# Attention plus feed-forward on one core: first values made beside keys and queries, queries split straight from PSUM, stacked copies moved in halves, last tiles in another order

## The chip, the cores and the metric

One core of a Trainium2 chip runs the whole program in one launch. Its engines are named as in the profile: PE (TensorE matmuls) and PEld (its weight loads), DVE (VectorE), ACT (ScalarE), POOL (GpSimd) and SP (SyncE, which here only issues DMAs). The metric is the device time of one execution in microseconds; lower is better.

## What is computed

The reference, cut to what matters (x is 2 x 1024 x 512, all float32, 16 heads of 32):

```python
qkv  = einsum('bsd,ed->bse', x, w_qkv) + b_qkv          # q, k, v: 2 x 16 x 1024 x 32
s    = einsum('bhqd,bhkd->bhqk', q, k) / sqrt(32)        # causal mask above the diagonal
out  = einsum('bhqk,bhkd->bhqd', softmax(s), v)          # heads side by side: 2 x 1024 x 512
x    = layernorm(x + einsum('bsd,ed->bse', out, w_out) + b_out)
h    = relu(einsum('bsd,hd->bsh', x, sign(up_weight)) * up_scale)           # 2048 wide
x    = layernorm(x + einsum('bsh,dh->bsd', h, sign(down_weight)) * down_scale * output_scale)
```

## The kernel before

**A planner writes the order.** Every step is a `task` with the engines that may run it, the modelled time it takes, a `place` (a due time, in units of one 128x128 block of attention scores) and the parts of tiles that it reads and writes. `Plan.schedule` (L133) walks through modelled time and, whenever an engine is free, gives it the ripe task with the lowest place. What it yields is one fixed order of instructions per engine. On the chip each engine runs its own list in that order and waits where an operand isn't there yet; SP's list of DMAs is such a queue too. A DMA takes one of 8 lanes (L50): the ninth is issued when the first has landed.

**Chunks.** There are 8 chunks `(b, e)`: batch b, and a group e of 4 heads (128 columns). A chunk has 8 query tiles of 128 rows; tile i looks at i+1 key blocks, so a chunk has 36 places (`STEP`, L496). While the attention of one chunk runs, `project` (L677) makes keys, queries and values of the next; the loop at L1285 sets the places.

**Projection.** `product` (L549) makes 128 features x 512 positions of keys or queries with 8 fp32 matmul passes (L554). Scores aren't multiplied in fp32: each number is split into a rounded part `hi` and a rest `lo` (both fp32r), and the four pairings of hi and lo are laid on top of each other over 128 partitions, once for each head (the "stacks"). Keys are split straight from PSUM, `split_keys` (L627): one ACT pass (L633) and one DVE pass (L638). Queries take three: `with_bias` (L570) writes a full copy with bias and scale on DVE (L575), and `split` (L612) makes hi and lo of it on POOL (L616, L621). `stack` (L645) then moves them with 16 DMAs for keys and 16 for queries, 1024 positions (128 KB) each; in the traces these are the lines `stacks<-wqkv`, issued by SP at L510. `values_of` (L585) makes the values, 512 positions at a time (L591).

**Attention.** `scores` (L810): matmuls into a PSUM tile of two banks (L847; the first four tiles of chunk 0 use plain fp32, L828), mask and row maximum on DVE (L885), exponential on ACT (L900), reciprocal on DVE (L912), scaling on POOL (L918). `transposes` (L930) turns blocks of 128x128 on PE (L939) and copies them to SBUF on ACT or DVE (L492, L494), into a ring `pt` of 60 blocks; a tile that doesn't fit before the ring's end starts at its beginning. `values` (L956) multiplies by the values (L968). After a batch's last chunk `output` (L1018) does the output projection (L1033) and the residual, and `normalise` (L1056) the layer norm (L1076).

**Start and end of the program.** `first_half` (L705) loads the first chunk's weights and the first 512 positions of x, in 128-row pieces c = 0 to 3, and multiplies keys and queries piece by piece (L755). Five tiny DVE copies (`hold`, L697) keep the values' weights and the second half of x from being issued before the first piece of x has landed. `second_half` (L786) makes the rest of chunk 0. The feed-forward (L1131) runs in 4 blocks of 512 rows; in the last one the output of a tile of 128 rows goes through L1225 (scale), L1234 (residual), L1242 and L1250 (statistics), L1257 (root), L1263 (reciprocal), L1268 (normalise) and a DMA of 256 KB. The last tile is made in two halves of 256 columns.

Of the kernel before, what the change touches and what calls it, by code (L numbers as in the profile page):

```python
# [11 lines left out]
F32R = mybir.dt.float32r  # L12
# [18 lines left out]
LAST = [0, 1, 2, 7, 6, 5, 4, 3]  # L31
# [43 lines left out]
class Plan:  # L75
# [8 lines left out]
    def ring(self, cls, n):  # L84

        self.classes[cls] = {"tiles": [], "next": 0, "ring": n, "live": [], "at": 0.0}

    def room(self, c, x):

        live, n = c["live"], x.blocks  # L90
        if not live:
            return 0
        head, tail = live[-1].slot + live[-1].blocks, live[0].slot
        if head > tail:
            return head if head + n <= c["ring"] else 0 if n <= tail else None
        return head if head + n <= tail else None
# [180 lines left out]
def kernel(  # L277
# [87 lines left out]
    def place_for(stack, name, n, kind=F32, side="left"):  # L365
# [22 lines left out]
        "hl": views(a_h, (2, S), F32R),  # L388
        "full": views(a_h, (TB,), at=2 * S),
# [70 lines left out]
    for cls, (_, n) in rings.items():  # L460
        plan.ring(cls, n)
# [25 lines left out]
    DMA = {"SP": (0.6, 0.6)}  # L487
# [43 lines left out]

    def load_w(b, e, place, parts, queue=DMA, after=()):
# [3 lines left out]
        for n in parts:  # L536
# [10 lines left out]
            )  # L547

# [21 lines left out]
    def with_bias(b, e, n, dst, parts, ps, at):  # L570
        bias = bqk[:, n * NC + e : n * NC + e + 1]
        if n == 0:
            plan.task(
                dve(0.74),
                lambda _: nc.vector.tensor_scalar(dst(), bank(ps), bias, scale, ALU.add, ALU.mult),  # L575
                at, [ps[0]], parts, label="bias",
            )
        else:
            plan.task(
                act(0.69),  # L580
                lambda _: nc.scalar.activation(dst(), bank(ps), AF.Identity, bias=bias),
                at, [ps[0]], parts, label="bias",
            )

    def values_of(b, e, v, t0, place):  # L585

        xt, w, ps = inputs[b], weights[b, e], new("f")
        for t in range(4):
            for c in range(NC):
                def fn(_, t=t, c=c):  # L590
# [10 lines left out]
                    [xt[c, t0], w[2]],  # L601
# [25 lines left out]
    def split_keys(b, e, hl, at, ps, place):  # L627

        bias = bqk[:, NC + e : NC + e + 1]
# [47 lines left out]
    def project(b, e, lo, mid, hi):  # L677
# [3 lines left out]
        for n in (1, 0):  # L681
            hl = new("hl")
            for t0 in range(0, S, TB):
                ps = product(b, e, n, t0, place)
                if n:
                    split_keys(b, e, hl, t0, ps, place() - FAST)
                else:
                    full = new("full")
                    with_bias(b, e, 0, lambda full=full: of(full), [full[0]], ps, place() - FAST)
                    split(hl, t0, lambda full=full: of(full), [full[0]], place())  # L690
            stack(st, n, hl, 0, 0, S, place, DMA)
        place = pace(mid, hi, 32)
# [3 lines left out]

    def hold(src, parts, dst, held):  # L697

        for d, h in zip(dst, held):
            plan.task(  # L700
                dve(0.15), lambda _, d=d: nc.vector.tensor_copy(d(), src()), -200, parts, [h],
                label="hold",
            )

    def first_half():  # L705
# [13 lines left out]
        for c, z, n in ((0, 1, 1), (0, 1, 0), (1, NC, 1), (1, NC, 0)):  # L719
            dma(  # L720
                -100,
                lambda c=c, z=z, n=n: of(w)[:, c:z, n, :],
                lambda c=c, z=z, n=n: w_qkvT[c * P : z * P, n * D : n * D + P].rearrange(
                    "(c p) f -> p c f", p=P
                ),
                64 * (z - c),
                writes=[w[n, k] for k in range(c, z)],
                queue=act_queue,
            )
            if n == 0 and c == 0:  # L730
                dma(-100, lambda: bqk, lambda: b_qkvP, 8, writes=[biases[0]], queue=act_queue)
        xt = inputs[0] = new("xT")
        for c in range(NC):
            dma(
# [6 lines left out]
        hold(  # L741
            lambda: of(xt)[:, 0, 0:1], [xt[0, 0]],
            [lambda: of(w)[:, 0, 2, 0:1], *[lambda c=c: of(xt)[:, c, TB : TB + 1] for c in range(NC)]],
            [w[2], *[xt[c, TB] for c in range(NC)]],
        )
        load_w(0, 0, -90, [2])
# [3 lines left out]
        both = {n: new("f") for n in (1, 0)}  # L750
        for c in range(NC):
            for n in (1, 0):
# [9 lines left out]
                    -50, [xt[c, 0], w[n, c]], updates=[both[n][0]], count=2,  # L762
                    label="ps",
                )
        for n in (1, 0):
            bias = bqk[:, n * NC : n * NC + 1]
            if n == 0:
# [3 lines left out]
                        rows(0), bank(both[0]), bias, scale, ALU.add, ALU.mult  # L771
# [11 lines left out]
        values_of(0, 0, v, 0, lambda units=0: -1)  # L783
        plain[0, 0] = kq, v

    def second_half():  # L786

        kq, v = plain[0, 0]
        st, hl = new("st"), new("hl")
        place = pace(-10, 6, 16 * 3)  # L790
        split(hl, 0, lambda: of(kq)[:, TB : 2 * TB], [kq[1]], -20)
        stack(st, 1, hl, 0, 0, TB, lambda: -20)
        ps = product(0, 0, 1, TB, place)
        split_keys(0, 0, hl, TB, ps, -10)
        stack(st, 1, hl, TB, TB, TB, lambda: -20)
        ps = product(0, 0, 0, TB, place)
        qh, full = new("hl"), new("full")
        with_bias(0, 0, 0, lambda: of(full), [full[0]], ps, -10)
        split(qh, 0, lambda: of(full), [full[0]], -10)
# [10 lines left out]
    def scores(b, e, i, heads, at):  # L810
# [86 lines left out]
        for j in range(G):  # L897
            plan.task(
# [31 lines left out]
    def transposes(i, heads, pr, at):  # L930
        blocks = [(j, ts(j * (i + 1) + k, P)) for j in range(len(heads)) for k in range(i + 1)]
        pt = new("pt", blocks=len(blocks))
# [198 lines left out]
    def feed_forward(up, dn, dsc, base):  # L1131
        UNIT = 2.0

        def block(tb):
# [80 lines left out]
            for t in range(TPB):  # L1215
# [3 lines left out]
                if very:  # L1219
                    at -= 23  # L1220
# [179 lines left out]
```

## Time and profile before

| | |
|---|---|
| median of 3 runs | 760.41 us (759.64 to 761.68) |
| the profiled execution | 761.84 us |
| its span, first to last instruction | 759.0 us |
| granted TensorE clock over the span | 0.997 |
| busy: PE, PEld, DVE, ACT, POOL | 745.2, 575.7, 476.3, 377.2, 267.3 us |
| SP's DMA issues of stacks | 224 of 128 KB, 48 of 64 KB |

How to read it: the profiled execution is one execution; 2.84 us of it lie outside the span. The attention part takes the first 505 us, the feed-forward the rest. In the groups of instructions the columns are line, engine, operation, output<-input, shapes and count, then busy time, mean ns of one, and the engine's idle time just before them with what ended it. In the timeline they are start, length of the merged group, engine, line, operation and count, and in brackets the idle time before it and who ended it. "SPq" is SP's queue of DMA issues.

### The profile page before, as it was taken

What the parts mean: (1) busy time and instruction counts of PE and PEld (TensorE: products, weight loads), DVE (VectorE), ACT (ScalarE), POOL (GpSimd) and SP (SyncE); (2) the same over time, 40 slices, a digit from 0 to 9 for tenths busy, and PEclk for the clock granted to TensorE, in tenths of its full rate; (3) what the DMA queues carried; (4) which work ended last, traced back from release to release, by engine and by line L of the source; (5) the groups of instructions that cost most, each with busy time, mean ns of one, the idle gap of its engine ahead of it and who ended that gap; (6) DMA issues with size and microseconds to landing.
All of it is one profiled execution on the core that took longest, in us unless ns stands there. A gap on an engine that the chain in (4) does not pass through costs nothing.

```text
span 759.0 us, 15486 instructions
## 1 busy us (share of the span) xinstructions
PE 745.2 (98%) x5890; PEld 575.7 (76%) x5890; DVE 476.3 (63%) x1146; ACT 377.2 (50%) x848; POOL 267.3 (35%) x333
## 2 busy tenths in 40 slices
PE   8999999999999999999999999999999999999995
PEld 4668869769757776886977977668787787778884
DVE  1657787787755767777778769744346337336525
ACT  1448776766642755687676767823222222222210
POOL 2416445445535453554544555520011002002005
PEclk9999999999999999999999999999999999999998
DMA  6577346057354125514505534241001001000101
GB/s 183 127 161 156 114 105 143 18 112 182 99 126 119 49 71 112 124 31 102 123 2 111 126 112 154 84 148 61 1 0 57 1 0 56 0 1 2 56 0 55
DMA packets 38216, 62.35 MB, mean 82 GB/s; under 512 B 6144, under 2 KB 18432, under 8 KB 38144
## 3 DMA queue, kind: packets, MB, share of 16 engines
q1 hardware_dynamic: 36912, 60.85, 31.1%
q8 instruction: 46, 0.75, 0.4%
q10 hardware_dynamic: 1232, 0.53, 0.3%
q14 instruction: 26, 0.21, 0.1%
HBM read 24.66 MB, written 4.19 MB: 38 GB/s over the span
## 4 chain that ended last, share of the span: by engine, by line
PE 90%; DVE 4%; DMA 2%; SPq 1%; POOL 1%; issue 1%; ACT 0%; POOLq 0%; ACTq 0%; DVEq 0%
PE s L939 15%; PE s L1153 15%; PE pd L1197 14%; PE s L554 13%; PE d L847 9%; PE s L968 8%; PE s L1033 7%; PE s L591 7%; SPq L510 1%; PE s L1101 1%; DMA xT<-in_xT 1%; PE d L828 1%; DVE x L1076 1%; DVE atT L1225 1%; DVE small L1242 1%
## 5 line engine op out<-in xcount | busy, mean ns | idle before, releaser
L918 POOL TENSOR_SCALAR probs<-probs,small 128x128 f32<-128x128 f32 (+7 forms) x256 | 189.0, 748 | 234.4 <-DVE small L912 160.6
L900 ACT ACTIVATE probs<-d,small 128x128 f32<-128x128 f32 (+7 forms) x256 | 189.3, 748 | 46.9 <-DVE small L912 17.7
L885 DVE CUSTOM_DVE_ANT_0 d<-d,mask 128x384 f32<-128x384 f32 (+7 forms) x200 | 173.3, 877 | 27.1 <-PE d L847 23.9
L939 PE MATMUL s<-ident,probs 128*128 128x128 f32 x1152 | 162.8, 273 | 1.3 <-DVE probsT L494 1.0
L939 PEld LDWEIGHTS s<-ident,probs 128*128 128x128 f32 x1152 | 135.7, 140 | 33.1 <-issue 22.4
L492 ACT COPY probsT<-s 128x512 f32<-128x512 f32 (+3 forms) x205 | 100.5, 519 | 117.6 <-PE s L939 113.8
L1153 PE MATMUL s<-xt,stacks 128*128 128x512 f32 x512 | 133.1, 400 | 0.0
L1197 PE MATMUL pd<-stacks,hid 128*128 128x512 f32 (+1 forms) x512 | 131.8, 392 | 0.6 <-DVE hid L1170 0.6
L1164 ACT ACTIVATE hf<-s,ups 128x512 f32<-128x512 f32 x64 | 44.0, 688 | 160.2 <-PE s L1153 158.2
L847 PE MATMUL d<-stacks 128*128 128x512 f32 (+3 forms) x368 | 121.3, 423 | 1.4 <-ACT probs L900 0.9
L554 PE MATMUL s<-xT,wqkv 128*128 128x512 f32 x240 | 118.6, 595 | 0.0
L1153 PEld LDWEIGHTS s<-xt,stacks 128*128 128x128 f32 x512 | 94.4, 188 | 23.7 <-issue 1.0
L1197 PEld LDWEIGHTS pd<-stacks,hid 128*128 128x128 f32 x512 | 92.7, 188 | 22.6 <-DVE hid L1170 1.5
L1170 DVE CAST hid<-hf 128x512 fp32r<-128x512 f32 x64 | 27.4, 428 | 121.7 <-ACT hf L1164 121.7
L494 DVE COPY probsT<-s 128x512 f32<-128x512 f32 (+3 forms) x140 | 82.2, 595 | 21.5 <-PE s L939 17.4
L847 PEld LDWEIGHTS d<-stacks 128*128 128x128 f32 x368 | 59.8, 190 | 36.9 <-issue 20.6
L591 PE MATMUL s<-wqkv,xT 128*128 128x128 f32 x512 | 75.3, 276 | 0.0
L591 PEld LDWEIGHTS s<-wqkv,xT 128*128 128x128 f32 x512 | 67.7, 191 | 7.2 <-issue 6.1
L968 PE MATMUL s<-probsT,v 128*32 128x128 f32 x2304 | 68.7, 274 | 0.0
L968 PEld LDWEIGHTS s<-probsT,v 128*32 128x32 f32 x2304 | 61.2, 110 | 9.6 <-DVE small L912 2.4
L1033 PE MATMUL s<-wout,atT 128*128 128x512 f32 x128 | 63.4, 594 | 0.0
L554 PEld LDWEIGHTS s<-xT,wqkv 128*128 128x128 f32 x240 | 39.4, 190 | 18.7 <-issue 17.4
(72 smaller groups left out, 521.9 us busy)
## 6 DMA issues: line engine op xcount, KB each, us to landing
stacks<-wqkv SPq DMA_DIRECT2D x224, 128.0 KB, 2.4
wqkv<-in_w_qkvT SPq DMA_DIRECT2D x22, 256.0 KB, 3.7
xT<-in_xT SPq DMA_DIRECT2D x16, 256.0 KB, 4.6
rows<-in_x SPq DMA_DIRECT2D x16, 256.0 KB, 2.6
raw<-in_up_wT SPq DMA_DIRECT2D x4, 1024.0 KB, 5.1
out<-atT SPq DMA_DIRECT2D x16, 256.0 KB, 2.0
stacks<-wqkv SPq DMA_DIRECT2D x48, 64.0 KB, 2.0
raw<-in_down_wT SPq DMA_DIRECT2D x2, 1024.0 KB, 5.1
```

Source lines behind the costliest of these rows:

```text
L492: nc.scalar.copy(dst, src)
L554: nc.tensor.matmul(of(ps).rearrange("p a b -> p (a b)"), lhsT=of(w)[:, c, n, :], rhs=of(xt)[:, c, t0 : t0 + TB], start=(c == 0), stop=(c = ...
L591: nc.tensor.matmul(of(ps)[:, t, :], lhsT=of(xt)[:, c, t0 + t * P : t0 + (t + 1) * P], rhs=of(w)[:, c, 2, :], start=(c == 0), stop=(c == NC ...
L847: nc.tensor.matmul(of(sc)[:, at0 : at0 + k1 - k0], lhsT=of(st)[:, 0, u, ts(i, P)], rhs=of(st)[:, 1, u, k0:k1], start=True, stop=True,)
L885: lambda _, j=j, some=some: nc.vector.tensor_tensor_reduce(some(), some(), keys(mask[:, S - N :], 0, N), scale=-1.0, scalar=LARGEST, op0=A ...
L900: lambda _, j=j: nc.scalar.activation(keys(of(pr), j, N), keys(of(sc), j, W), AF.Exp, bias=of(nm)[:, j : j + 1], scale=sign, accum_out=of( ...
L918: lambda _, j=j: nc.gpsimd.tensor_scalar(of(pr)[:, j * N : (j + 1) * N], of(pr)[:, j * N : (j + 1) * N], of(sums)[:, j : j + 1], 1.0, ALU. ...
L939: lambda _, k=k, c=c, tp=tp: nc.tensor.transpose(of(tp)[:, k, :], of(pr)[:, c], ident),
L968: nc.tensor.matmul(of(to)[ts(u, HD), n, :], lhsT=of(v)[:, k, ts(u, HD)], rhs=of(pt)[:, ts(c + k, P)], start=(k == i), stop=(k == 0),)
L1033: lambda _, c=c: nc.tensor.matmul(bank(py), lhsT=of(a)[:, c, :], rhs=of(wout)[:, c, :], start=(c == 0), stop=(c == NC - 1),),
L1153: lambda _, f=f, c=c, n=n, pu=pu: nc.tensor.matmul(of(pu), lhsT=of(up)[:, f // TPB, c, ts(f % TPB, P)], rhs=of(xt)[:, n, c, :], start=(c = ...
L1197: lambda _: nc.tensor.matmul(of(to)[:, d0:d1], lhsT=of(h)[:, ts(t, P)], rhs=of(dn)[:, f // 4, f % 4, d0:d1], start=(f == 0 and n == 0), st ...
```

## The change

- `first_half`: weights come by piece c, keys' and queries' together; piece 0 goes over ACT's queue, pieces 1 to 3 over SP's just ahead of the same piece of x. The values of the first 512 positions are multiplied piece by piece too, into a bank of their own, in places after keys and queries. `hold` is gone; the values' weights of pieces 1 to 3 follow the last piece of x, then x's second half.
- Queries are split from PSUM as keys are (`split_bank`: ACT, then DVE). The factor 1/sqrt(32) is put into the queries' weights by one POOL pass for each chunk (`scaled`) and into the bias once. `with_bias` is gone.
- `hl` holds 512 positions, and there are three of them; `stack` is called for each 512 positions: 64 DMAs of 64 KB for a chunk in place of 32 of 128 KB.
- During chunk 0, chunk 1's values come first (places 0 to 12), its keys and queries in places 4 to 24, its weights earlier.
- The ring `pt` may wrap inside a tile; a group of 4 blocks that lies across its end is copied in two pieces.
- The first batch's 8 layer-norm steps move into chunk 4, each behind a tile's exponential.
- The last chunk's tiles run in the order 2, 7, 6, 5, 4, 3, 1, 0 (before: 0, 1, 2, 7, 6, 5, 4, 3).
- In the last feed-forward block, each tile's closing steps have places of their own (the tile before the last closes after the last); the normalising step is on DVE, the residual add on DVE or POOL as the planner finds, and the last tile's two halves are normalised and sent separately, the first over ACT's queue.

```diff
-LAST = [0, 1, 2, 7, 6, 5, 4, 3]
+LAST = [2, 7, 6, 5, 4, 3, 1, 0]
...
     def room(self, c, x):
+        if c["wraps"]:
+            return head % c["ring"] if sum(y.blocks for y in live) + x.blocks <= c["ring"] else None
...
-        "hl": views(a_h, (2, S), F32R),
-        "full": views(a_h, (TB,), at=2 * S),
+        "hl": views(a_h, (2, TB), F32R),
...
-    DMA = {"SP": (0.6, 0.6)}
+    DMA = {"SP": (0.64, 0.64)}
...
+    def scaled(w, place, parts):
+        plan.task(
+            pool(0.69),
+            lambda _: nc.gpsimd.tensor_scalar(
+                of(w)[:, :, 0, :], of(w)[:, :, 0, :], scale, 1.0, ALU.mult, ALU.mult
+            ),
+            place, updates=[w[p] for p in parts], label="scale",
+        )
...
     def load_w(b, e, place, parts, queue=DMA, after=()):
+            if n == 0:
+                scaled(t, place + 10, [0])
...
-    def split_keys(b, e, hl, at, ps, place):
-        bias = bqk[:, NC + e : NC + e + 1]
+    def split_bank(b, e, n, hl, at, ps, place):
+        bias = bqk[:, n * NC + e : n * NC + e + 1]
...
-    def project(b, e, lo, mid, hi):
+    def project(b, e, lo, mid, hi, values=None):
         for n in (1, 0):
-            hl = new("hl")
             for t0 in range(0, S, TB):
+                hl = new("hl")
                 ps = product(b, e, n, t0, place)
-                if n:
-                    split_keys(b, e, hl, t0, ps, place() - FAST)
-                else:
-                    full = new("full")
-                    with_bias(b, e, 0, lambda full=full: of(full), [full[0]], ps, place() - FAST)
-                    split(hl, t0, lambda full=full: of(full), [full[0]], place())
-            stack(st, n, hl, 0, 0, S, place, DMA)
-        place = pace(mid, hi, 32)
+                split_bank(b, e, n, hl, 0, ps, place() - FAST)
+                stack(st, n, hl, t0, 0, TB, place)
+        place = pace(mid if values is None else values, hi, 32)
...
+        weight(0, 1, 1, act_queue)
+        weight(0, 0, 1, act_queue)
+        dma(-100, lambda: bqk, lambda: b_qkvP, 8, writes=[biases[0]], queue=act_queue)
+        weight(0, 2, 1, act_queue)
         for c in range(NC):
+            if c:
+                weight(c, 0, 2, DMA)
             dma(-100, lambda c=c: of(xt)[:, c, :TB], lambda c=c: xT[ts(c, P), :TB], 256, ...)
-        hold(...)
-        load_w(0, 0, -90, [2])
+        for c in range(1, NC):
+            weight(c, 2, 1, DMA)
         load_x(0, -80, [TB])
...
-                    -50, [xt[c, 0], w[n, c]], updates=[both[n][0]], count=2,
+                    c - 50, [xt[c, 0], w[n, c]], updates=[both[n][0]], count=2,
+            for t in range(TB // P):
+                plan.task(
+                    {"PE": (0.218, 0.218)},
+                    lambda _, c=c, t=t: nc.tensor.matmul(
+                        of(vs)[:, t, :], lhsT=of(xt)[:, c, ts(t, P)], rhs=of(w)[:, c, 2, :],
+                        start=(c == 0 and t == 0), stop=(c == NC - 1 and t == TB // P - 1),
+                    ),
+                    c - 40, [xt[c, 0], w[2, c]], updates=[vs[0]], count=2, label="ps_v",
+                )
...
     def second_half():
+        scaled(weights[0, 0], -30, [(0, c) for c in range(NC)])
...
+        if b and e == 0:
+            normalise(b - 1, base + 18, [marks[b, e, (NQ + t) // 2] for t in range(NQ)])
...
+            if at == 0:
+                load_w(nb, ne, base - 25, [2, 1, 0], after=[latest["x"]])
+                project(nb, ne, base + 4, base + 24, base + 12, base)
+            else:
+                load_w(nb, ne, base - 15, [1, 0, 2])
+                project(nb, ne, base, base + MID * STEP, base + HI * STEP)
...
+                if final:
+                    at += 3 * t - 30
+                later = at + (20 if final and t + 2 == TPB else 0)
...
-                    pool(0.69) if final and not very else dve(0.546),
+                for k, (_, d0, d1) in enumerate(columns(t)):
+                        dve(0.546 if whole else 0.32),
...
+                    dma(at, ..., reads=[y[d0]],
+                        queue=DMA if whole or k else {"ACT": (0.65, 0.65)}, label="out")
-        ADDS = {False: [pool(1.264)] * 3 + [dve(0.692)], True: [pool(1.264)] * 3}
+        either = {**dve(0.692), **pool(1.264)}
+        ADDS = {False: [pool(1.264)] * 3 + [dve(0.692)], True: [either] * 3}
```

## The prediction

> **What bounds the kernel now.** I read the page's first section, then the table of PE's waits, then the timeline at the start, at one change of chunk and at the end.
>
> ```profile
> PE 745.2 (98%) x5890; PEld 575.7 (76%) x5890; DVE 476.3 (63%) x1146; ACT 377.2 (50%) x848; POOL 267.3 (35%) x333
> ```
> ```profile
> PE s L712 <- DVE x L708: 1.0, 1, 1.0
> PE s L755 <- DMA xT<-in_xT: 1.0, 1, 1.0
> PE s L939 <- DVE probsT L494: 1.0, 2, 0.7
> PE d L847 <- ACT probs L900: 0.9, 2, 0.7
> PE pd L1197 <- DVE hid L1170: 0.6, 2, 0.3
> PE d L847 <- DMA stacks<-wqkv: 0.5, 1, 0.5
> ```
> PE is the bound nearly everywhere: its waits (columns: total, times, longest) come to under 6 us. A busy PE may still stand behind an operand, so I laid each matmul's start against the back-to-back spacing of its own form (0.429 us for an fp32 pass of 512 columns, 0.109 for 128, 0.232 for an fp32r pass, 1.72/4 and 3.41/120 in merged groups, and so on). Those spacings sum to 729.6 us of work; from the first matmul (1.04) to the last one's end (751.2) there are 20.6 us of slack. 8.1 of these lie before 54 us, some 10 in pieces of 0.1 where PE changes its kind of matmul, 3.2 between 432 and 486, under 0.4 after 540. The change removes no PE work: 240 + 16 products, 512 value matmuls and all scores stay. So it can win in three places alone: the start, a few stalls in the middle, and the 7.8 us after PE's last matmul.
>
> The start:
> ```profile
> 4.62 1.98 PE L755 MATMUL s<-xT,wqkv 128*128 128x512 f32 x4
> 6.88 1.96 PE L755 MATMUL s<-xT,wqkv 128*128 128x512 f32 x4 [0.28 <-DMA wqkv<-in_w_qkvT]
> 9.85 3.70 PE L755 MATMUL s<-xT,wqkv 128*128 128x512 f32 x8 [1.01 <-DMA xT<-in_xT]
> ```
> PE stands before 6.88 and before 9.85, where the fourth piece of x lands at 9.81: it was the ninth DMA and left only when the first had landed (4.59).
>
> A change of chunk, and the end:
> ```profile
> 102.81 25.93 SPq L510 DMA_DIRECT2D stacks<-wqkv  x32
> 132.29 0.33 PE L847 MATMUL d<-stacks 128*128 128x128 f32 x1 [0.46 <-DMA stacks<-wqkv]
> ```
> ```profile
> 749.97 1.19 DVE L1234 TENSOR_TENSOR atT<-atT,xT 128x256 f32<-128x256 f32 x1
> 750.87 4.35 POOL L1268 TENSOR_SCALAR atT<-atT,small 128x512 f32<-128x512 f32 x2
> 751.68 0.46 DVE L1225 SCALAR_TENSOR_TENSOR atT<-s,osc,v 128x256 f32<-128x256 f32 x1
> 752.47 0.40 DVE L1234 TENSOR_TENSOR atT<-atT,xT 128x256 f32<-128x256 f32 x1
> 754.21 0.55 DVE L1268 TENSOR_SCALAR atT<-atT,small 128x512 f32<-128x512 f32 x1
> ```
> The next chunk's first score waited for its last stack (landed 132.24). At the end POOL normalises two tiles until 755.22; SP's third output leaves at 755.24 behind it, the fourth at 755.67 though DVE had its rows ready at 754.76. It lands at 757.93, and 1.1 us of closing semaphores end the span.
>
> **The change part by part.** The sum is made against the profiled execution (761.84 us: span 759.0 and 2.84 around it), which is 1.43 above the median of 760.41; I subtract the same sum from the median.
>
> *Start.* The work on the first 512 positions is 16 passes x 0.429 = 6.9 us for keys and queries and 32 x 0.109 = 3.5 us for values. Today it ends at 13.4 and the values follow, so it is worth 16.9. In the change, piece 0's values fill the wait for later pieces: from 4.62 without a gap it is done at 15.0, **-1.9**. Does it starve? Three DMAs (piece 2 of x, weights 3, piece 3) now leave after the first landing, and 64 KB more (piece 0's values' weights) go ahead; today such a DMA took 4.59 to 9.81. Put piece 3 a lane later (issue near 5.5, landing 10.7): PE has by then 5.2 us of keys and queries and 0.87 of values behind it, exactly the 6.1 us since 4.62, and 1.7 + 2.6 are left: 15.0 again. Each us later than that costs one; ends -0.6 and -1.9. The query's bias (L770, today 13.59) and the first scores (15.20) come by as much earlier.
>
> *Queries from PSUM.* Per block of 512 it takes off DVE 0.749 (L575), POOL 0.623 + 1.278 (L616, L621) and puts on ACT 0.692 (L633) and DVE 0.742 (L638): over 15 blocks DVE is level, POOL -28.5, ACT +10.4. The weights' scaling costs POOL 8 x 0.69 (the 512-wide row of L918, 692 ns). ACT is busy 38 of 54 us in an attention stage, so the 1.4 per chunk hide; without that cover they cost up to 10.4. The query product now waits for POOL's scaling: queued behind it on POOL are the probabilities (L918). The weights land a chunk ahead (77.43 issue for products after 104), and its place is 10 after the load, so I take nothing.
>
> *Stacks in halves.* 224 issues become 448. Issues of 64 KB went out every 0.634 us (12.40 to 33.19, 32 of them), those of 128 KB took hardly longer, so SP gets 142 us more: 64 x 0.634 = 40.6 of a 54.9 us chunk. What it moves: in chunk 1 the first key half was split by 95.88 (ACT 93.88, L638 at 95.13), yet its stack waited for the second until 102.81. In halves SP can begin near 95: keys until 115.3, first query half (product ready at 107.6) until 125.4, landed 127.4; second until 135.6, landed 137.6, which tile 4 asks for at 148.2. The wait at 132.29 (0.58 with its pipeline) goes: **-0.6**. [...] The trace's rows are 2.0 us to landing for 64 KB against 2.4 for 128 KB, at one issue per 0.634 us in either case: no DMA engine limits here, SP's issuing does.
>
> *Chunk 0 and 1.* SP issues stacks from 12.4 on: 48 x 0.634 + 3 weights x 0.57 end near 44.6 (today 46.42), then chunk 1's 64 with six other DMAs: first query half landed about 77.5 (today all at 76.58), second 88, asked for by tile 4 at 93.46 less the start's gain. PE has between 77 and 88 the transposes and values of tiles 6 and 7 to do. Chunk 1's values (7.0 us), early now, fill PE before 46. I take zero; the second rival prices it.
>
> *Layer norm of batch 0.* Eight DVE steps from 300.04 to 305.20 held up L885, and PE stood 0.85 at 306.6 and 307.5. Spread behind four tiles' exponentials they fit (DVE 76% busy): **-0.8**.
>
> *Last tiles, ring.* Slack of 0.85 at 451.96, 0.91 at 479.29 and 0.47 at 490.36 belongs to the order of today. No row shows the new order, so it may cost as much as it can win: -2.2 to +2.2. Ending with one-block tiles shortens the chain into the feed-forward; I take **-0.6**. The ring's wrap frees room rarely, and a split copy costs one extra 128-wide copy (0.27) now and then on DVE or ACT: inside these ends.
>
> *End.* DVE after the last matmul: today 751.68 to 754.17 for scale, add, statistics, root, reciprocal. Then two halves of about 0.33 in place of 0.55, and no POOL. If the last tile's first half (0.48 + 0.40 + 0.41) still stands in front, the reciprocal is done at 754.1 and the last issue goes at 754.85; if not, near 754.1. Against 755.67 that is -0.8 to -1.5: **-1.1**. The 256-wide add took 1.19 beside POOL and 0.40 later, so POOL adds left there by the planner shift this by 0.8 either way. [...]
>
> Sum: -1.9 - 0.6 - 0.8 - 0.6 - 1.1 = **-5.0**: the profiled execution 756.8, the median 760.4 - 5.0 = **755.4**.
>
> **Rivals.**
>
> *SP becomes the bound (slower).* Place: each change of chunk. If stacks can't begin before today's 102.81, keys end at 123.1, the first query half lands at 135.2, and the score that waited 0.58 waits 3.5: +3.0 for each of six changes, 18 - 5 = +13, **773**. It decides from a first stack issue later than 99.8 in chunk 1 (99.8 + 30.4 + 2.0 = 132.24). Against it: the split half at 95.88. For it: SP's list is in order, and a row load or weight load that waits (SP waited 36.9 us behind L591) blocks the stacks. Chance 0.12.
>
> *The start's gain is eaten.* Stacks are issue-bound from 12.4 to 75 already; if the first scores of chunk 1 (76.97 today, 0.4 after the landing) set PE's pace, the 1.9 is lost: -3.1, **757.3**. Against it: PE stood nowhere between 54 and 108 (slack 0.9). Chance 0.20.
>
> *The last chunk trips.* Tile 7, now second, needs the second query half. Shifted by the same sums (first key half 394.33, L633) it lands at 437.8, some 3 us after a tile 2 that starts at 431.8 has given up its two PSUM tiles. PE loses up to 2.8, the 0.6 isn't won, and the end half its gain: -1, **759.4**. Chance 0.10.
>
> **How the numbers follow.** About 0.3%, 2.3 us, is what a measurement of this kernel can tell from no change: under 758.1 is faster. The likeliest case (0.58) gives 755.4, its good ends -1.9 - 0.6 - 0.8 - 2.2 - 1.9 = -7.4, **753.0**. The upper end takes in the second and third rival and the bad ends of the middle: **760.2**. Faster: 0.58 + 0.18 of the second rival = 0.76; same: 0.10 + 0.02 = 0.12; slower 0.12.
>
> **What would show it.** Right: L755 and the value matmuls without a wait from 4.6 to 15; first scores near 13.3; chunk 1's stacks starting before 99.8 and no wait of L847 for stacks; L1076 no longer in one run near 300; the last output issued before 755 minus the gains ahead of it; PE's busy work unchanged. Wrong: PE rows that name stacks or the scaled weights as releaser, SP issues without gaps from one chunk into the next, or new PE waits between 430 and 505.

## The result: slower by 0.9%, and the profile after

| | before | after |
|---|---|---|
| median | 760.52 us (759.64 to 761.68, 6 runs) | 767.39 us (766.68 to 769.41, 6 runs) |
| ratio | | 1.0094, 95% interval 1.0079 to 1.0108 |
| profiled execution, its span | 761.84, 759.0 us | 769.41, 767.5 us |
| granted clock over the span | 0.997 | 0.991 |

The prediction said 755.4 us, 0.76 for faster. A few executions that ran far slower than the others of the same kernel (771 to 1866 us) are left out of all comparisons below; the profiled execution of the kernel with the order and the end together was one, so only its time is used.

The page's first section and the table of PE's waits, after (columns as before: total, times, longest; two short rows left out). Lines from first_half on have moved: L755 is now L757, L847 is L863, L939 is L963, and the product of L554 is L579.

```profile
PE 751.1 (98%) x5890; PEld 578.7 (75%) x5890; DVE 478.7 (62%) x1146; ACT 388.0 (51%) x868; POOL 234.6 (31%) x305
```
```profile
PE s L579 <- DMA wqkv<-in_w_qkvT: 4.1, 1, 4.1
PE d L863 <- DMA stacks<-wqkv: 2.4, 2, 1.9
PE s L709 <- DVE x L705: 1.0, 1, 1.0
PE s L963 <- POOL rows L1049: 0.7, 1, 0.7
...
PE s L963 <- ACT probsT L505: 0.5, 1, 0.5
```

PE does the same 5890 matmuls, 729.6 us of work by the spacings of the prediction. Two waits are new: one of 4.1 us for a *weight load*, one of 1.9 us for stacks. The slack of PE by that method is 30.7 us, before it was 20.6. Of the 10.1 more, 6.4 lie between 108 and 162 us (8.2 against 1.8) and 2.5 between 432 and 486 (5.6 against 3.2); the stretch before 54 us has only 0.6 less (7.5 against 8.1). The largest piece of the rest, some 2 us, lies between 216 and 270 us: PE waits 0.55 us before 240.36 and 0.73 before 245.37, the second time behind POOL's L1049, which had itself stood 3.5 us for a row load that SP issued at 240.80, among stacks. After PE's last matmul the program takes 6.2 us where it took 7.8. So +10.1 - 1.6 = +8.5, the difference of the two spans; the medians differ by 6.9 only: the profiled execution after was the slowest of its six, and before 2.84 us lay outside the span, after 1.9.

The start, in PE's timeline of the changed kernel (start, length, engine, line, operation, count):

```profile
5.04 4.42 PE L757 MATMUL s<-xT,wqkv 128*128 128x512 f32 x8
9.30 0.83 PE L770 MATMUL s<-wqkv,xT 128*128 128x128 f32 x6
...
13.63 2.84 PE L770 MATMUL s<-wqkv,xT 128*128 128x128 f32 x24
16.40 0.50 PE L844 MATMUL d<-probsT 32*128 32x128 f32 x8
```

There is no bracket: nothing is waited for, as forecast. But the work ends at 16.4 us, not 15.0, and the first scores (L844) start at 16.40, where they started at 15.20 before. The first eight passes start at 5.04 instead of 4.62 and take 0.55 us each on average instead of 0.43: the clock records grant full speed from 6.69 us in this execution, from 4.06 in the one before. The first two passes start 0.86 us apart, those from 6.72 on 0.43.

The first change of chunk that goes wrong, PE's timeline and then that of SP's queue. First before, where chunk 3's weights went out 61 us ahead of its first product, then after:

```profile
77.43 6.53 SPq L510 DMA_DIRECT2D wqkv<-in_w_qkvT  x3
...
138.19 1.02 PE L554 MATMUL s<-xT,wqkv 128*128 128x512 f32 x2
```
```profile
135.71 1.04 PE L963 MATMUL s<-ident,probs 128*128 128x128 f32 x8
140.85 2.04 PE L579 MATMUL s<-xT,wqkv 128*128 128x512 f32 x2 [4.10 <-DMA wqkv<-in_w_qkvT]
142.69 1.91 PE L963 MATMUL s<-ident,probs 128*128 128x128 f32 x8
```
```profile
59.77 1.65 SPq L523 DMA_DIRECT2D wqkv<-in_w_qkvT  x3
61.51 76.02 SPq L523 DMA_DIRECT2D stacks<-wqkv  x112
137.57 1.71 SPq L523 DMA_DIRECT2D wqkv<-in_w_qkvT  x3
```

SP issues 112 stacks in one run of 76 us, 0.68 us each on average, and the three parts of chunk 3's weights stand behind them in its list. They go out at 137.57; PE was ready for them at 136.75. And what follows runs at half pace: the group of eight transposes takes 1.91 us after the wait, 1.04 ahead of it. The view by stretches of time shows why (stretch, length, busy time and count of PE, PEld, DVE, ACT, POOL, then granted clock, DMA share, GB/s), first of before, then of after:

```profile
136.00:147.00 11.00, 11.00 (x169) 8.90 (x167) 7.39 (x22) 7.12 (x25) 4.39 (x11) 1.00 0.10 25
```
```profile
136.00:147.00 11.00, 6.90 (x29) 4.13 (x31) 4.58 (x11) 4.78 (x20) 3.04 (x7) 0.69 0.83 237
447.00:451.00 4.00, 4.00 (x32) 3.05 (x36) 1.72 (x4) 1.85 (x3) 1.15 (x2) 0.57 0.36 104
```

The clock is granted at half from 139.81 for 6.83 us, from within the first wait on, and again from 447.01 for 3.41 us, right behind the second. In this execution the wait of 4.1 us costs some 7.1 us in all, the one of 1.9 us some 3.9. This is the second one, in the last chunk:

```profile
444.14 0.82 PE L963 MATMUL s<-ident,probs 128*128 128x128 f32 x6
446.90 1.09 PE L863 MATMUL d<-stacks 128*128 128x512 f32 x2 [1.94 <-DMA stacks<-wqkv]
```

Tile 7, second in the new order, asks for the second query half; the stacks of its first heads release this line, the last one landed at 448.73. The end went as forecast, a little better, DVE and ACT's queue in the timeline:

```profile
761.42 0.75 DVE L1258 TENSOR_TENSOR atT<-atT,xT 128x256 f32<-128x256 f32 x2
...
763.64 0.74 DVE L1294 TENSOR_SCALAR atT<-atT,small 128x256 f32<-128x256 f32 x2
764.08 0.35 ACTq L523 DMA_DIRECT2D out<-atT  x1
```

Two adds of 256 columns together take 0.75 us with POOL idle; before, one took 1.19 beside POOL's add (L1234) and one 0.40 beside its normalising (L1268). The last output lands 5.0 us after PE's last matmul.

### The profile page after: what moved, and what is told of

The parts are those of the page before. It is cut to its first block, busy times and chain, and to the rows that moved or that the text cites. A ratio compares the mean times of both kernels' runs of the same rounds, so it can differ in the third digit from the quotient of the medians.

```text
span 767.5 us, 15846 instructions
## 1 busy us (share of the span) xinstructions
PE 751.1 (98%) x5890; PEld 578.7 (75%) x5890; DVE 478.7 (62%) x1146; ACT 388.0 (51%) x868; POOL 234.6 (31%) x305
## 4 chain that ended last, share of the span: by engine, by line
PE 87%; DVE 5%; SPq 4%; DMA 2%; issue 1%; ACT 1%; POOL 0%; DVEq 0%; ACTq 0%
PE s L1176 15%; PE s L963 14%; PE pd L1220 14%; PE s L579 11%; PE s L990 8%; PE d L863 8%; PE s L1055 7%; PE s L601 6%; SPq L523 4%; DMA stacks<-wqkv 1%; PE s L757 1%; PE s L1124 1%; DVE small L1266 1%; DVE d L901 1%; DVE atT L1249 1%
## 5 line engine op out<-in xcount | busy, mean ns | idle before, releaser
L934 POOL TENSOR_SCALAR probs<-probs,small 128x128 f32<-128x128 f32 (+7 forms) x256 | 189.3, 749 | 259.6 <-DVE small L928 193.7
L963 PE MATMUL s<-ident,probs 128*128 128x128 f32 x1152 | 164.0, 274 | 1.5 <-POOL rows L1049 0.7
L963 PEld LDWEIGHTS s<-ident,probs 128*128 128x128 f32 x1152 | 136.2, 141 | 35.3 <-issue 22.4
L863 PE MATMUL d<-stacks 128*128 128x512 f32 (+4 forms) x368 | 121.8, 425 | 2.6 <-DMA stacks<-wqkv 2.4
L579 PE MATMUL s<-xT,wqkv 128*128 128x512 f32 x240 | 120.3, 602 | 4.1 <-DMA wqkv<-in_w_qkvT 4.1
L507 DVE COPY probsT<-s 128x512 f32<-128x512 f32 (+3 forms) x138 | 80.6, 594 | 33.1 <-PE s L963 30.8
L863 PEld LDWEIGHTS d<-stacks 128*128 128x128 f32 x368 | 60.2, 192 | 37.4 <-issue 19.5
L601 PE MATMUL s<-wqkv,xT 128*128 128x128 f32 x480 | 72.0, 278 | 0.0
L601 PEld LDWEIGHTS s<-wqkv,xT 128*128 128x128 f32 x480 | 64.6, 193 | 7.8 <-issue 6.7
L579 PEld LDWEIGHTS s<-xT,wqkv 128*128 128x128 f32 x240 | 39.9, 193 | 22.5 <-issue 21.5
```

The lines of the kernel that those rows point to most:

```text
L579: nc.tensor.matmul(of(ps).rearrange("p a b -> p (a b)"), lhsT=of(w)[:, c, n, :], rhs=of(xt)[:, c, t0 : t0 + TB], start=(c == 0), stop=(c = ...
L601: nc.tensor.matmul(of(ps)[:, t, :], lhsT=of(xt)[:, c, t0 + t * P : t0 + (t + 1) * P], rhs=of(w)[:, c, 2, :], start=(c == 0), stop=(c == NC ...
L863: nc.tensor.matmul(of(sc)[:, at0 : at0 + k1 - k0], lhsT=of(st)[:, 0, u, ts(i, P)], rhs=of(st)[:, 1, u, k0:k1], start=True, stop=True,)
L934: lambda _, j=j: nc.gpsimd.tensor_scalar(of(pr)[:, j * N : (j + 1) * N], of(pr)[:, j * N : (j + 1) * N], of(sums)[:, j : j + 1], 1.0, ALU. ...
L963: lambda _, k=k, c=c, tp=tp: nc.tensor.transpose(of(tp)[:, k, :], of(pr)[:, c], ident),
```

## The experiments

The runs of the kernel before in the four batches have medians of 760.43, 760.28, 760.64 and 760.36 us; each experiment's ratio is to its own batch.

### Are the two waits the loss? Weights earlier, old order of last tiles, both

Three kernels are the changed one with the first, the second and both of these edits:

```diff
-                load_w(nb, ne, base - 15, [1, 0, 2])
+                load_w(nb, ne, base - 40, [1, 0, 2])
```
```diff
-LAST = [2, 7, 6, 5, 4, 3, 1, 0]
+LAST = [0, 1, 2, 7, 6, 5, 4, 3]
```

Weights earlier. 

> The changed kernel with one place altered: the weights of chunks 2 to 7 are due 40 places before their chunk's projection, not 15, so SP's list has chunk 3's weights ahead of chunk 2's 64 stacks. Queue theory: the 4.1 us wait before 140.85 goes with the half clock behind it, -7.1 us, the wait near 447 stays: about 760.3. Rival (SP is short of issue time as such, whatever the order): stacks come 2 us later in their turn and PE waits for them instead, 764 to 767.

Measured 761.59 us (10 runs), 1.0013 [0.9998, 1.0027]. The wait for weights is gone, and the median is 5.8 us below the changed kernel's. The wait for the second query half is still there, 2.1 us, and in this profiled execution no half clock followed it (0.999 granted over the span). A wait of 1.25 us for an exponential, before 200.39, is new.

Old order. 

> The changed kernel with the last chunk's tiles in the former order 0, 1, 2, 7, 6, 5, 4, 3. Queue theory: tile 7 asks for the second query half some 6 us later, the 1.9 us wait before 446.90 goes with its 3.4 us of half clock, -3.8, while 0.9 at the former stalls of that chunk may return; the wait near 141 stays: 763.6 to 764.5. Rival (the new order is better by itself and the wait moves to another operand): 767 or more.

Measured 766.34 us (9 runs, 763.15 to 769.65), 1.0078 [1.0057, 1.0099]. The wait in the last chunk is gone. The wait for weights was 2.9 us in the profiled execution, the one of 763.15 us, and no half clock followed it there (0.999 granted over the span). The spread of 6.5 us over the runs goes with the granted clock that each run has on record: 0.999 in that of 763.15 us, 0.996 or 0.997 in those of 764.63 to 766.74, 0.993 or 0.994 in those of 768.45 to 769.65. So the longer runs had the lower clock; behind which wait it fell, only a trace could show, and one run alone has one. The median lies outside both of the ranges expected.

Both. 

> The changed kernel with both edits together: weights due 40 places ahead, and the last chunk's tiles in the former order. If the two long waits and their half clock are all that went wrong with the forecast, 767.4 - 7.1 - 3.8 = 756.5. If the middle of the kernel never had the 2 us that I had booked there (the slack left in the trace with early weights, its wait near 441 taken off, is about 20.5 us, the same as before the change), only the end's 1.6 us are left: about 759. No row of PE should wait for weights or stacks over 1 us.

Measured 761.01 us (11 runs), 1.0014 [1.0005, 1.0024]. Neither wait is left, the slack is 21.2 us, and the time is that of before, hardly more. So the two waits are some 6 of the 7 us lost. And since the new end alone is worth 1.8 (below), nothing of what was booked for start and middle is left in sum even without them. One place where it goes is the new wait that comes with the earlier weights, here again 1.25 us, before 198.86; before 54 us its slack is some 1.7 less than in the kernel before.

### What does the half clock cost? Filling the wait

The changed kernel, with ten fp32 passes of constants put ahead of chunk 3's first key product, into its own PSUM bank before it starts there. They are extra work; no result uses them.

```diff
+                if (b, e, n, t0, c) == (0, 3, 1, 0, 0):
+                    for _k in range(5):
+                        nc.tensor.matmul(bank(ps), lhsT=ident, rhs=mask[:, :TB], start=True, stop=True)
                 nc.tensor.matmul(
```

> The changed kernel with ten extra fp32 passes of 0.43 us in front of the key product of chunk 3, on constants, into the bank that the product overwrites: PE computes nothing of use in the 4.1 us in which it would wait for that product's weights. Clock theory (the idle wait makes the chip halve PE's clock for the next 6.8 us): the weights come no earlier, but the half clock from 139.8 to 146.6 goes, 767.4 - 3.4 = 764. Rival (the small stalls after 140.85 are late operands, the clock is chance): 767 to 768, or up to 4 more if the passes end after the weights have landed.

Measured 764.84 us (4 runs), 1.0063 [1.0048, 1.0077]. PE's timeline and the same stretch as above:

```profile
137.97 4.46 PE L581 MATMUL s<-mask,ident 128*128 128x512 f32 x10
142.26 1.02 PE L582 MATMUL s<-xT,wqkv 128*128 128x512 f32 x2
```
```profile
136.00:147.00 11.00, 11.00 (x107) 7.32 (x110) 5.96 (x13) 6.14 (x24) 4.34 (x8) 1.00 0.79 224
```

Doing useless work instead of idling made the kernel 2.6 us faster. The product starts later, at 142.26 instead of 140.85, but at full clock. The DMA share is as high as before (0.79 against 0.83), so it isn't the transfers that slowed PE there. In 108 to 162 us the slack and the useless passes together are 5.3 us against 8.2. The 2.6 us of the medians may not be this stretch's alone: in this execution the wait in the last chunk was shorter too (1.0 us, before 444.41), and no half clock followed it (1.00 granted in 447 to 451 us).

### Whole stacks in the changed kernel

```diff
+            hl = new("hl")
             for t0 in range(0, S, TB):
-                hl = new("hl")
                 ps = product(b, e, n, t0, place)
-                split_bank(b, e, n, hl, 0, ps, place() - FAST)
-                stack(st, n, hl, t0, 0, TB, place)
+                split_bank(b, e, n, hl, t0, ps, place() - FAST)
+            stack(st, n, hl, 0, 0, S, place)
```

(`hl` holds 1024 positions again, and there is one.)

> The changed kernel with its stacks moved whole again (1024 positions, 128 KB, 32 DMAs a chunk); all else of the change stays. Queue theory (SP can't issue 64 stacks a chunk in time, the weights of a later chunk and the last query half come late): both long PE waits (4.1 us before 140.85, 1.9 us before 446.90) go, and with them the half-clock stretches behind them; 767.4 - 7.1 - 3.8 = about 756.5, granted clock 0.997 or more. Rival (the new order of chunk 0 and 1, with the values first, makes the waits): the wait for weights near 140 stays, 762 to 766. Rival (the last tiles' order by itself costs): a wait stays near 447.

Measured 763.45 us (10 runs), 1.0035 [1.0024, 1.0046]: 3.9 better than the change, 7 short of the 756.5 expected. Both long waits are gone; but each chunk from 162 to 432 us now has 2.4 to 2.8 us of slack, about 1 to 2 more than in the kernel before, much of it in short waits:

```profile
PE s L963 <- ACT probsT L505: 2.9, 5, 0.8
PE s L963 <- DVE probsT L507: 2.0, 5, 0.7
...
PE s L963 <- DVE wqkv L648: 0.6, 2, 0.3
```

These are transposes that wait for a PSUM bank, the last row for one that a query product held. My theory of the halves alone had no place for that; the next two runs test it.

### Halves alone, and queries from PSUM alone

The kernel before with `hl` of 512 positions (two buffers) and a `stack` call for each, and all else as it was:

```diff
             for t0 in range(0, S, TB):
+                hl = new("hl")
...
-            stack(st, n, hl, 0, 0, S, place, DMA)
+                stack(st, n, hl, t0, 0, TB, place, DMA)
```

> The kernel before with one part of the change alone: stacks in halves of 512 positions (64 DMAs of 64 KB a chunk), two half-size buffers in place of one; queries still by way of the full copy and POOL, the old order of chunks 0 and 1, the old last tiles. Queue theory: the halves by themselves make SP late, a later chunk's weights queue behind 64 stacks, PE waits for them or for stacks and loses the clock: 764 to 770. Rival (the halves are harmless, the new order of chunk 0 and 1 does it): 758.5 to 761.

Measured 773.21 us (4 runs), 1.0158 [1.0135, 1.0181]; the slack before 54 us is 14.8 us instead of 8.1. SP's queue:

```profile
11.89 31.18 SPq L510 DMA_DIRECT2D stacks<-wqkv  x48
43.12 3.52 SPq L510 DMA_DIRECT2D wqkv<-in_w_qkvT  x6
```

Chunk 1's weights went out at 33.23 before; now they stand behind all 48 stacks. No wait of PE names them, for chunk 1's first product stands later in PE's list, at 46.67 instead of 36.45. Until then PE has too little else: it waits 1.24 us for stacks before 42.68 and 1.36 for an exponential before 45.20. The granted clock over the span is 0.993, where the kernel before has 0.997. So the kind is that of the queue theory, weights late behind stacks; the size is beyond its range. The slack before 54 us is about half of the loss; the rest lies in pieces up to 505 us that were not followed up.

The kernel before with queries split from PSUM, whole stacks and one buffer:

```diff
-                if n:
-                    split_keys(b, e, hl, t0, ps, place() - FAST)
-                else:
-                    full = new("full")
-                    with_bias(b, e, 0, lambda full=full: of(full), [full[0]], ps, place() - FAST)
-                    split(hl, t0, lambda full=full: of(full), [full[0]], place())
+                split_bank(b, e, n, hl, t0, ps, place() - FAST)
```

> The kernel before with one part alone: queries split from PSUM, scale in their weights; stacks whole, one buffer of 1024 positions for hi and lo, as before. Buffer theory: with no full copy in between, a query product keeps its PSUM bank until the keys' 16 stacks have left the only buffer (some 11 us), the other users of the four banks are short of one, and PE stands as it did with the changed kernel's stacks made whole (slack of 2.7 us a chunk, not 0.9): 6 chunks of 1.8 us, 765 to 771. Rival (the split is cheap and POOL's relief helps): 759.5 to 761.

Measured 769.92 us (4 runs), 1.0117 [1.0104, 1.013]: in the range of the buffer theory. PE's waits, and one change from keys to queries in the timeline:

```profile
PE s L935 <- DVE probsT L493: 3.9, 7, 1.1
PE s L935 <- ACT probsT L491: 2.7, 5, 0.8
```
```profile
117.62 1.27 ACT L629 ACTIVATE wqkv<-s,bqk 128x512 fp32r<-128x512 f32 x2
...
119.57 0.30 PE L935 MATMUL s<-ident,probs 128*128 128x128 f32 x1 [0.31 <-DVE wqkv L634]
```

Both query splits start together at 117.62, right when the last key stack has landed (117.02): until then the only buffer was the keys', and two query products sat in PSUM banks that the transposes share. The first was complete near 108.9 and stood there for 8.7 us; before, `with_bias` (L575) took such a product at 107.59, as soon as it was done. The extra passes of ACT and DVE don't do it by themselves: the changed kernel has them too, and its transposes waited 0.5 us for ACT's copies. So splitting from PSUM needs more buffers than one (two whole ones were not run), and the change's three half buffers need twice the issues: each part alone is worse than the whole change.

### The start alone, and with chunk 0's new order

The kernel before with the changed `first_half` only.

```diff
+        for c in range(1, NC):
+            weight(c, 2, 1, DMA)
...
+                    c - 40, [xt[c, 0], w[2, c]], updates=[vs[0]], count=2, label="ps_v",
```

> The kernel before with the start alone taken over (weights by piece, values beside keys and queries, nothing held back). Start theory: PE stands 1.6 us less before 54 us, 758.8. Rival (the gain is eaten: the key bias comes later, SP's first stack issue moves from 12.4 to about 14.4, and SP's chain of stacks sets the pace of chunk 0 and 1): 760 to 761.5.

Measured 766.87 us (4 runs), 1.0091 [1.0078, 1.0104]. PE's timeline, the stretch behind it, and SP's queue:

```profile
50.84 1.61 PE L862 MATMUL d<-stacks 128*128 128x320 f32 x4 [2.81 <-DMA stacks<-wqkv]
```
```profile
50.80:57.50 6.70, 5.22 (x15) 3.69 (x16) 4.70 (x11) 4.36 (x10) 1.34 (x2) 0.50 0.48 116
```
```profile
14.36 21.18 SPq L510 DMA_DIRECT2D stacks<-wqkv  x32
35.58 2.81 SPq L510 DMA_DIRECT2D wqkv<-in_w_qkvT  x5
38.49 12.78 SPq L510 DMA_DIRECT2D stacks<-wqkv  x16
```

The first stack goes out at 14.36, 2 us later than before (12.40), and the last query stack at 51.27, 4.9 us later: the keys' bias that feeds it (ACT, 12.97 instead of 11.01) comes later, since passes for values now stand ahead of the last key passes, and the first eight passes, from 5.31 us, took 4.15 us, where the kernel before has a group of eight in 3.70. In the execution with the old order the first stack went out at 13.36. So SP starts later, and PE meets a wait of 2.8 us, with a granted clock of 0.50 from 50.80 to 57.50. The time is worse than both theories expected; the kind is that of the rival.

Then the same, with the changed kernel's order of chunk 0 as well:

```diff
+                load_w(nb, ne, base - 25, [2, 1, 0], after=[latest["x"]])
+                project(nb, ne, base + 4, base + 24, base + 12, base)
```

> The kernel before with the new start and the new order of chunk 0 (chunk 1's weights earlier, its values first, its keys and queries in places 4 to 24); stacks whole, queries by way of the full copy. The start alone cost 6.6 us: PE ran out of work and stood 3 us before 50.84 for the last query stacks. Filling theory: chunk 1's values, early, are the work that was missing; no wait over 1 us before 60 us, 759 to 761. Rival (SP's chain of stacks, begun 2 us later and now with three weight loads in front, sets the pace whatever PE has to do): 764 or more.

Measured 761.03 us (10 runs), 1.0009 [0.9999, 1.0018]. Between 2 and 60 us the table of PE's waits is empty. The values of chunk 1 fill PE while SP catches up, which takes the loss of 6 us away; a gain isn't there.

### The parts that work: the end, the order of the last tiles, both

The kernel before with the changed closing steps of the feed-forward:

```diff
-                if very:
-                    at -= 23
+                if final:
+                    at += 3 * t - 30
+                later = at + (20 if final and t + 2 == TPB else 0)
```

> The kernel before with the closing steps of the last feed-forward block alone taken over (normalising on DVE, adds on DVE or POOL, the last tile sent in two halves, the tile before it closed last). From PE's last matmul to the end the trace had 7.8 us before the change and 6.2 after it: 760.4 - 1.6 = 758.8. Rival (the last DMA's landing and the closing semaphores set the end whatever DVE does): 760.4.

Measured 758.52 us (11 runs), 0.9976 [0.9968, 0.9985]: -1.8. PE's last matmul to the end takes 6.2 us here too.

With the layer norm's spread added:

```diff
-                at, [m[0], m[1]], updates=[y[t]], label="ln",
+                at, [m[0], m[1]], updates=[y[t]], label="ln", after=behind[t : t + 1],
```

> The kernel before with two parts taken over: the new closing steps of the last feed-forward block, and the first batch's eight layer-norm steps spread over chunk 4. The closing steps alone gave 758.5. If the 0.85 us that PE stood near 306 behind that run of eight DVE steps goes: 757.7. Rival (DVE is only busy elsewhere, PE waits as long in another place): 758.5.

Measured 758.48 us (5 runs), 0.9966 [0.9954, 0.9978]. Each against the kernel before of its own batch, this is -2.2 and the closing steps alone -1.8: the spread's 0.4 lies within the intervals and can't be told from nothing. In the trace the stall before 306.60 us is gone, the one before 307.5 is still there (0.35, before 0.42), and one of 0.42 before 245.21 is new.

The order of the last tiles alone in the kernel before, the LAST line above the other way round. 

> The kernel before with the last chunk's tiles in the order 2, 7, 6, 5, 4, 3, 1, 0 and nothing else. If the wait near 447 in the changed kernel is the doubled issues' alone, whole stacks (landed near 431.7) are in time and the order costs nothing: 759.3 to 760.8. Rival (a large tile in second place outruns its operands or DVE in any case): 762 to 764.

Measured 759.16 us (12 runs), 0.9981 [0.997, 0.9992]: -1.5. The slack from 432 to 486 us fell from 3.2 to 1.9, and that from 486 to 505 is 0.3. With whole stacks the second query half is there in time.

The order and the end together, without any other part. 

> The kernel before with the two parts that won alone: the last chunk's new tile order (759.2 alone) and the new closing steps (758.5 alone). They act at 430 to 505 us and behind PE's last matmul, so the gains should add: 760.4 - 1.3 - 1.8 = 757.3. Rival (the order moves work that the closing steps need, or part of a gain was chance): 758.5.

Measured 756.86 us (4 runs), 0.995 [0.9936, 0.9964]: -3.5, about the sum of the two (-1.8 and -1.5). It beats the kernel before and the changed one.

### Does the planner only need the right price of a DMA?

```diff
-    DMA = {"SP": (0.64, 0.64)}
+    DMA = {"SP": (0.69, 0.69)}
```

> The changed kernel with one number of the planner altered: SP's modelled time for a DMA issue 0.69 us, as the trace has it over long runs, not 0.64. If the waits come from the model's error (112 stacks x 0.04 = 4.5 us, about the 4.1 us wait), the planner now orders around them: 762 to 764. Rival (SP's list is simply full: it works without a pause from 14 to 144 us, and the weights stand behind the stacks by their due place): the wait near 141 stays or moves, 766 to 769.

Measured 766.79 us (3 runs), 1.0074 [1.0057, 1.0092]. With this price the planner moved the loss: waits of 3.8 us in four pieces near 80 us behind POOL's scaling of the probabilities (L934). SP's queue is nearly without a pause from 13.9 to 93.6 us. Chunk 2's weights now stand behind 90 stacks and go out at 79.70 (59.77 in the changed kernel), and PE has no product of keys or queries between 75 and 88 us, where the changed kernel has several. A higher price alone doesn't mend the order: SP's list is full there.

## Why the prediction was wrong, step by step

| step | booked | measured |
|---|---|---|
| change of chunk (weights' place) | 0 | about +7.1 in the trace; 5.8 from the median when taken away |
| last tiles | -0.6 | -1.5 alone; with halves a wait worth +3.9 |
| start | -1.9 | -0.6 in the trace after, -1.6 in that with the old order; +6.6 alone, +0.7 with chunk 0's new order |
| stacks in halves | -0.6 | +12.8 alone |
| queries from PSUM | 0 | +9.3 alone |
| layer norm | -0.8 | -0.4, not told from 0 |
| end | -1.1 | -1.6 in the traces, -1.8 alone |

**The step that failed** is the one on SP's list across chunks: "I take zero" under "Chunk 0 and 1", and before it "The weights land a chunk ahead". I laid SP's list out in time only up to 88 us and took the later weights' issue time from the trace of before; the 77.43 named there is the issue of chunk 3's weights, whose products begin at 138.19, not 104. Their place in the list (57) is behind chunk 2's stacks (36 to 52); with 64 issues a chunk instead of 32, and a backlog that began at 14.36 us and not at 12.4, everything behind them moves: they went out at 137.57, and PE waited 4.1 us. The sum was also short on time: an issue does take 0.634 us at the median, but the long runs average 0.68 to 0.69, since some in them take longer (eight of the 112 intervals are 0.9 to 1.8 us), which is 3 to 4 us more over a chunk's 64. SP's backlog from the start was in view ("issue-bound from 12.4 to 75 already"), and I didn't carry it on to chunk 3. A sign of being wrong that the prediction lists came true: SP issued without gaps from one chunk into the next.

**The first rival** named the right engine and even the right operands ("a row load or weight load ... blocks"), with the roles reversed: it is the stacks that block the weights. It priced six changes of chunk by late stacks; there the stacks came early, as in the main forecast (the wait at 132.29 is gone; one of 0.43 us before 81.85 is left). One change with late weights was enough.

**A term was missing**: the clock. Every wait was priced at its own length. The trace of before has no long wait, so no row of it showed what follows one; the changed kernel's trace shows 6.83 us at half clock with the wait of 4.1 and 3.41 with that of 1.9, which adds some 3.0 and 2.0 us to them there.

**The last tiles**: the third rival's mechanism, with a landing forecast at 437.8 and measured at 448.73. The sum had the first of the 64 stacks near 395 (437.8 less 64 x 0.634 and 2.0 to landing); it went out at 403.01, and the 64 issues took 44.3 us, not 40.6. Most of the 10.9 us between the two landings is the whole execution's lateness by then (the first key half was split at 402.30 instead of 394.33, 8.0 us); some 3 us are SP's. Its price of "up to 2.8" missed the clock again.

**The start**: PE's side came as worked out, no waits, but for the first scores: forecast near 13.3, they started at 16.40, behind the values (15.40 in the execution with the old order). And its first two passes, and the matmuls ahead of them, ran before the clock rose at 6.69 us. In the execution with the old order the slack before 54 us is 6.5, so the change holds most of the 1.9 there; that the clock makes this difference was not shown. With the start alone, what sets the pace near 50 us is SP, though. The second rival ("the start's gain is eaten") is right in kind and too small: a PE that comes early to a full list waits, and pays for the wait.

**Queries from PSUM**: the engine costs did hide, as said (0.5 us of waits for ACT's copies in the changed kernel). What I didn't count is how long a PSUM bank is held. In the changed kernel the three half buffers pay for that, so this cost doesn't show; it shows that the halves can't be left out without another buffer.

**Right**: the work of PE is unchanged; the end. Of the layer norm's two stalls one went, and PE met another at 245.2, so that slack was not a sum of independent pieces. **Open**: the wrap of the ring was not run alone, and where the start's gain goes is followed only in part.

The time to issue a stack isn't small here: 0.63 us per issue at the median against about 2.0 to landing, with 112 issues in a row while earlier transfers run, so issuing is the bound.

## What to carry to other kernels

When a change doubles the number of DMAs on an in-order queue, go through the whole list behind them and ask of each entry when it is needed now, small weight loads above all, and carry the backlog forward until it is gone. Don't price a wait of PE at its own length alone: here one of 1.94 us cost some 3.9 and one of 4.1 some 7.1, with half clock behind them, while none followed one of 2.9. If a wait can't be removed, filling it with any matmuls can help, as it did here once (764.84 us against 767.39). Test parts of a change alone only where no part pays for another: here the split from PSUM needed the buffers that the halves bring, and the two parts that needed no other were the gain.

## What the hardware showed that I had not expected

In the changed kernel's trace the clock is granted at half twice before PE's last matmul: from 139.81 us (6.83 us long, wait of 4.1) and from 447.01 (3.41, wait of 1.94). PE's next longest waits there past its first matmul, 0.73 us before 245.37 and 0.55 before 240.36, have no half clock behind them. With the start alone the granted clock is 0.50 from 50.80 to 57.50 us, behind a wait of 2.8, and 1.00 from 57.50 to 64.00. In the kernel before, where PE's longest wait past its first matmul is 1.01 us, it is 1.00 from 4.06 us to PE's last matmul. Half clock did not follow waits of 2.9 us (old order) and 2.1 us (weights earlier): 0.999 is granted over the span in both executions, and 3.41 us at half would take 0.002 off 1. What sets these two apart from the wait of 1.94 us was not shown.

A stack of 64 KB takes SP as long to issue as one of 128 KB: the median from one issue to the next is 0.63 us for both in the kernel before. So moving a chunk's stacks in halves, 64 issues for 32, doubles SP's work here.
